# Adding the own part of a graph layer in PSUM after the division, with deeper buffers and a larger allowance in the instruction planner

## Chip, cores, metric

One core of a Trainium2 chip (trn2). The metric is the device time of one execution in microseconds (us).

## The reference, cut to what matters

The network has 32 graphs of 512 nodes with 128 features. `adj` is 0/1, symmetric, with ones on the diagonal. Four layers follow one another, each on a layer norm and ReLU of `x`, each added to `x`: masked attention (layer 0), a graph convolution whose weights come from an LSTM of 128 steps (layer 1), a four-step message passing (layer 2), and a linear graph layer (layer 3).

```python
# layer 2, one of four steps; input of step 2: [f2, f1]; of step 3: [f3, f1, f0]
src_agg  = einsum('bjv,bij->biv', nodes @ ws + bs, _l2norm(adj, 2))
dst_agg  = einsum('bjv,bji->biv', nodes @ wd + bd, _l2norm(adj, 1))
self_rep = nodes @ wn + bn                      # the "own" part
return tanh(concatenate([src_agg, self_rep, dst_agg], 2) @ wu + bu)
```

As `adj` is symmetric and 0/1, both aggregations divide by the same norm, the root of the degree. The kernel folds `ws`, `wd`, `wn` with `wu` at the start, so a step is `tanh(A y / norm + own + bias)`, where `A y` is the aggregation and `own` one product with a folded weight.

## The kernel before

The kernel records every operation with a rank, its reads, its writes and a guess of its duration. A planner then simulates the engines and fixes the order in which each engine gets its instructions. This order is static, fixed when the kernel is built. An engine's wait for the next one in line shows in the trace as idle time: in the kernel before, TensorE's waits came to 55.2 us in 50 cases between 620 and 1600 us. The planner adds an allowance between a producer on one engine and its consumer on another: `HOP`, or `HOP_PE` where the consumer is TensorE. LSTM steps have ranks below `URGENT` and a fixed small allowance of their own.

```python
class Plan:
    HOP, HOP_PE, HOP_URGENT, URGENT = 0.25, 0.8, 0.14, 1000
    # in put(o), for each engine e that can do operation o:
    hop = self.HOP_URGENT if o.rank < self.URGENT else self.HOP_PE if e == "PE" else self.HOP
    o.ready[e] = max([0.0] + [d.end + (hop if d.engine != e else 0.0) + d.gap for d in o.deps])

BUFS = {"a": 2, "ar": 4, "x": 5, "xn": 4, "y": 6, "gs": 4, "norm0": 3, "norm1": 3,
        "n0": 3, "n1": 3, "n2": 3, "n3": 3, "m0": 3, "m1": 3, "m2": 3, ...}
# tags in this list hand out their buffers in the order in which tiles were made:
plan = Plan(BUFS, ("ar", "x", "norm0", "norm1", "n0", "n1", "n2", "n3", "m0", "m1", "a"))
```

Pass 1 does the attention of the last 128 nodes of each graph (ranks from 10,000). The LSTM then runs with pass 2, the attention of the other nodes, beside it (20,000). The "rest" is layers 1 to 3 (30,000). Keys and queries wait in DRAM between pass 1 and pass 2. Layer 2 of one batch:

```python
for i, nch in enumerate(L2_CHUNKS):                    # 1, 1, 2, 3 chunks
    m = new(f"m{min(i, 2)}", (P, N), ...)
    DVE(..., nc.vector.tensor_mul(m.t, nodes[i].t, norm_row.t))   # node x norm
    ...  # py = bias + nodes @ folded weight; parts = py split into two fp32r parts
    def own():                                          # first into the bank
        for c, n in order[1:] + order[:1]:
            nc.tensor.matmul(pa.t, wf[:, W_F[i] + c, 1, :], scaled[n].t, start=..., stop=False)
    PE(R, nch * t_mm(N), own, [scaled[n] for n in CHUNKS[i]], [pa])
    def got():                                          # aggregation, eight matmuls
        ...  nc.tensor.matmul(pa.t, parts.t[:, j, k, :], ar.t[:, j, :], start=False, ...)
    PE(R, 8 * t_r(N), got, [parts, ar], [pa])
    DVE(R, t_dve(N), ... nc.vector.tensor_mul(pa.t, pa.t, inv_row.t))     # x 1/norm
    ACT(R, 0.5, ... tanh(pa + bias))
```

## Time and profile before

| | us |
|---|---|
| median of 4 runs | 1697.99 (1695.79 to 1701.61) |
| pass 1 ends (its last f_seq starts) | 251.6 |
| last LSTM tanh | 614.7 |
| last matmul of pass 2 (f_po) | 606.2 |
| granted TensorE clock, whole run | 0.981 |

The prediction below shows the lines that it rests on. Here are the stages, with borders at the end of pass 1 and at the last tanh of the LSTM. The columns are: stretch, length, busy us (and instructions) of PE (TensorE matmuls), PEld (its weight loads), DVE (VectorE), ACT (ScalarE) and POOL (GpSimd), granted clock, DMA share, GB/s. The tile names in later lines: f_pa is the PSUM bank in which aggregation and own part meet, f_py the product of nodes and folded weight, f_y its split parts, f_n the tanh, f_nb the row of norms, f_ar the squared adjacency; f_pf and f_hT_d belong to layer 3, f_po to pass 2, f_z, f_th and f_seq to the LSTM.

```profile
0.00:251.60 251.60, 213.58 (x1372) 171.19 (x1373) 139.86 (x648) 132.67 (x256) 86.88 (x240) 0.99 0.62 202
251.60:614.70 363.10, 358.04 (x2434) 301.93 (x2433) 200.19 (x958) 125.60 (x393) 53.34 (x103) 0.98 0.56 166
614.70:1694.80 1080.10, 1006.13 (x6147) 810.13 (x6147) 649.02 (x1787) 468.29 (x1079) 177.25 (x345) 0.98 0.14 44
700.00:1560.00 860.00, 813.40 (x5000) 655.31 (x5001) 522.11 (x1428) 386.22 (x891) 145.35 (x284) 0.99 0.15 47
```

The last row is the steady part of the rest. A batch has 193 TensorE instructions there (counted in the program), so 5000 of them in 860 us make one batch per 860 x 193 / 5000 = 33.2 us. I use this rate below, with 189 instructions for kernels that have the change.

### The profile page before, as it was taken

To read this page: it belongs to the slowest core of one execution; us is meant where nothing else is said; L and a number is where in the kernel's file an instruction comes from. 1 tells how busy PE (TensorE), PEld (TensorE's weight loads), DVE (VectorE), ACT (ScalarE), POOL (GpSimd) and SP (SyncE) were. 2 spreads that over 40 slices of the span, in tenths; PEclk is the share of its full clock that TensorE was granted. 3 is DMA by queue.
4 is the path that set the end of the run, shared out by engine and by line. 5 is a ranking of instruction groups with operands and counts; after the bars stand their busy time and mean duration, and the time that the engine had idled before them with its cause. 6 is when DMAs were issued, how large, how long until landed. Compare 5 with 4: busy or idle time off the path is not lost. (4 is left out here: it accounts for less than half of the span.)

```text
span 1694.8 us, 27758 instructions
## 1 busy us (share of the span) xinstructions
PE 1577.8 (93%) x9949; PEld 1283.3 (76%) x9949; DVE 989.1 (58%) x3392; ACT 726.6 (43%) x1727; POOL 317.5 (19%) x688
## 2 busy tenths in 40 slices
PE   5998999999999989999999899999999999999995
PEld 4777778888888878777777777777778777777774
DVE  4655655555555666566565665665756566565753
ACT  3565543333333354454444444444444444444431
POOL 3333321011111131121121111111211121121100
PEclk9999999999999989999999999999999999999997
DMA  7555665555555630111111111111301111011100
GB/s 254 188 186 175 199 214 175 157 163 155 162 156 157 200 130 26 38 51 38 63 50 38 63 38 50 63 38 38 100 13 38 50 63 63 13 50 38 38 7 15
DMA packets 144955, 159.06 MB, mean 94 GB/s; under 512 B 8612, under 2 KB 111140, under 8 KB 144808
## 3 DMA queue, kind: packets, MB, share of 16 engines
q1 hardware_dynamic: 143936, 155.42, 29.3%
q8 instruction: 80, 1.31, 0.3%
q10 hardware_dynamic: 872, 1.78, 0.3%
q14 instruction: 67, 0.55, 0.1%
HBM read 117.26 MB, written 39.91 MB: 93 GB/s over the span
## 5 line engine op out<-in xcount | busy, mean ns | idle before, releaser
L1283 PE MATMUL f_pa<-f_ar,f_y 128*128 128x512 f32 x1024 | 285.0, 421 | 13.9 <-DVE f_y L1156 9.5
L1283 PEld LDWEIGHTS f_pa<-f_ar,f_y 128*128 128x128 f32 x1024 | 188.1, 189 | 84.7 <-issue 23.7
L1276 PE MATMUL f_pa<-f_m,f_wf 128*128 128x512 f32 x448 | 215.8, 600 | 1.1 <-DVE f_m L1259 0.6
L1267 PE MATMUL f_py<-f_wf,f_n 128*128 128x128 f32 x1280 | 175.8, 276 | 10.5 <-ACT f_n L1287 10.4
L1267 PEld LDWEIGHTS f_py<-f_wf,f_n 128*128 128x128 f32 x1280 | 165.0, 192 | 19.8 <-ACT f_n L1287 14.0
L1287 ACT ACTIVATE f_n<-f_pa,f_bcol 128x512 f32<-128x512 f32 x128 | 87.7, 686 | 205.8 <-DVE f_pa L1285 205.8
L1085 PEld LDWEIGHTS f_z<-f_seq,f_w 128*128 128x128 f32 x1016 | 126.2, 194 | 26.5 <-DVE f_seq L1106 22.2
L1085 PE MATMUL f_z<-f_seq,f_w 128*128 128x32 f32 x1016 | 134.8, 277 | 5.1 <-DVE f_seq L1106 3.3
L1156 DVE TENSOR_TENSOR f_y<-f_py,f_y 128x512 fp32r<-128x512 f32 x128 | 87.8, 687 | 81.4 <-ACT f_y L1155 81.1
L1285 DVE TENSOR_TENSOR f_pa<-f_pa,f_norm 128x512 f32<-128x512 f32 x128 | 88.6, 693 | 79.3 <-PE f_pa L1283 79.2
L943 ACT ACTIVATE f_xn_c<-f_x,f_sh_c,f_rs_c 128x128 f32<-128x128 f32 x118 | 53.1, 487 | 156.4 <-DVE f_sh_c L948 138.8
L1276 PEld LDWEIGHTS f_pa<-f_m,f_wf 128*128 128x128 f32 x448 | 76.7, 193 | 50.8 <-issue 46.4
L1138 PE MATMUL f_po<-f_v,f_e 128*128 128x129 f32 x768 | 115.1, 285 | 0.0
L1138 PEld LDWEIGHTS f_po<-f_v,f_e 128*128 128x128 f32 x768 | 101.7, 195 | 11.5 <-PE f_s L1128 0.4
L1128 PE MATMUL f_s<-f_q,f_k 128*128 128x384 f32 x256 | 102.2, 498 | 0.5 <-PE f_pd L1054 0.5
L1155 ACT CAST f_y<-f_py 128x512 fp32r<-128x512 f32 x128 | 74.0, 579 | 59.4 <-PE f_py L1267 59.3
L1259 DVE TENSOR_TENSOR f_m<-f_n,f_norm 128x512 f32<-128x512 f32 x96 | 66.0, 687 | 42.9 <-ACT f_n L1287 42.9
L1089 ACT ACTIVATE f_th<-f_z 128x128 f32<-128x128 f32 x128 | 35.4, 277 | 129.5 <-PE f_z L1085 125.0
L1237 DVE SCALAR_TENSOR_TENSOR f_junk<-f_a,f_aT 128x512 bf16<-128x512 f32 x128 | 86.5, 675 | 1.6
L1132 DVE TENSOR_TENSOR f_e<-f_e,f_a 128x384 f32<-128x384 f32 x128 | 69.0, 548 | 30.5 <-ACT f_e L1131 29.8
L1267 PE MATMUL f_py<-f_wf,f_hT_c 128*128 128x128 f32 x512 | 83.3, 275 | 0.0
L1096 DVE SCALAR_TENSOR_TENSOR f_cu<-f_th,f_c 128x32 f32<-128x32 f32 x127 | 24.4, 192 | 99.2 <-ACT f_th L1089 98.5
(189 smaller groups left out, 3118.8 us busy)
## 6 DMA issues: line engine op xcount, KB each, us to landing
f_a<-in_adj_dram SPq DMA_DIRECT2D x32, 1024.0 KB, 5.1
f_a<-in_adj_dram SPq DMA_DIRECT2D x32, 768.0 KB, 5.6
f_dv<-f_v SPq DMA_DIRECT2D x32, 258.0 KB, 3.6
f_v<-f_dv SPq DMA_DIRECT2D x32, 258.0 KB, 2.8
f_x<-in_x_dram SPq DMA_DIRECT2D x32, 256.0 KB, 3.1
f_al<-in_adj_dram SPq DMA_DIRECT2D x32, 256.0 KB, 3.2
f_dk<-f_kT SPq DMA_DIRECT2D x32, 256.0 KB, 3.2
f_k<-f_dk SPq DMA_DIRECT2D x32, 256.0 KB, 2.7
```

Source lines behind the costliest of these rows:

```text
L1085: nc.tensor.matmul(z.t[:, k, q, :], w[:, W_HH + q, :], seq[:, t - 1, :], start=False, stop=True, skip_group_check=True)
L1128: PE(R, t_mm(NR), lambda s=s, j=j: nc.tensor.matmul(s.t, kT.t[:, bass.ts(j, P)], qT.t, start=True, stop=True), [kT, qT], [s])
L1132: DVE(R, t_dve(NR), lambda e=e, j=j: nc.vector.tensor_mul(e.t, e.t, a.t[:, j, :]), [a], [e])
L1138: nc.tensor.matmul(po.t[:, t, :], es[j].t[:, bass.ts(t, P)], v.t[:, j, :], start=(j == 0), stop=(j == NT - 1))
L1155: ACT(rank, t_act(N), lambda: nc.scalar.copy(parts.t[:, :, 0, :], src.t), [src], [(parts, 0)])
L1156: DVE(rank, t_dve(N), lambda: nc.vector.tensor_sub(parts.t[:, :, 1, :], src.t, f32(parts.t[:, :, 0, :])), [src, (parts, 0)], [(parts, 1)])
L1237: DVE(R + 2, 0.7, lambda tp=tp, j=j: nc.vector.scalar_tensor_tensor(junk, a.t[:, j, :], 1.0, flat(tp.t), OP.mult, OP.not_equal, accum_out= ...
L1267: nc.tensor.matmul(py.t[:, j, :], nodes[n].t[:, bass.ts(j, P)], wf[:, W_F[i] + c, 0, :], start=False, stop=(c == nch - 1), skip_group_chec ...
L1276: nc.tensor.matmul(pa.t, wf[:, W_F[i] + c, 1, :], scaled[n].t, start=(c == (1 if len(order) > 1 else 0)), stop=False)
L1283: nc.tensor.matmul(pa.t, parts.t[:, j, k, :], ar.t[:, j, :], start=False, stop=(k == 1 and j == NT - 1))
L1285: DVE(R, t_dve(N), lambda pa=pa: nc.vector.tensor_mul(pa.t, pa.t, inv_row.t), [inv_row], [pa])
L1287: ACT(R, 0.5, lambda pa=pa, n=n, i=i: nc.scalar.activation(n.t, pa.t, AF.Tanh, bias=bcol[:, i : i + 1]), [pa], [n])
```

## The change

The intent: skip the products of every node with the norm by adding the own part to what VectorE has divided, give the freed space to deeper buffers, and plan with more slack. Its core:

```diff
-    HOP, HOP_PE, HOP_URGENT, URGENT = 0.25, 0.8, 0.14, 1000
+    HOP, HOP_PE, HOP_URGENT, URGENT = 0.25, 1.2, 0.14, 1000
-    BUFS = {"a": 2, "ar": 4, "x": 5, "xn": 4, "y": 6, "gs": 4, "norm0": 3, "norm1": 3, "n0": 3, ... "m0": 3, "m1": 3, "m2": 3, ...
+    BUFS = {"a": 2, "ar": 5, "x": 6, "xn": 5, "y": 7, "gs": 5, "inv": 4, "n0": 4, "n1": 4, "n2": 4, "n3": 4, ...
@@ pass 1 and pass 2: keys and queries in one tile, in the buffers "ar" of the squared adjacency
-        qT = new("m0", (P, N), f"f_qT_{b}")
-        kT = new("m1", (P, N), f"f_kT_{b}")
+        kq = new("ar", (P, 2, N), f"f_kq_{b}")
-        DMA(R + 5, 192, lambda: nc.sync.dma_start(dq.t, qT.t[:, :NR]), [qT], [dq])
-        DMA(R + 5, 256, lambda: nc.sync.dma_start(dk.t, kT.t), [kT], [dk])
+        DMA(R + 5, 448, lambda: nc.sync.dma_start(dkq.t, flat(kq.t)[:, : N + NR]), [kq], [dkq])
@@ layer 2
-            DVE(R, t_dve(N), lambda m=m, i=i: nc.vector.tensor_mul(m.t, nodes[i].t, norm_row.t), ...)
-            PE(R, nch * t_mm(N), own, [scaled[n] for n in CHUNKS[i]], [pa])
             PE(R, 8 * t_r(N), got, [parts, ar], [pa])          # now opens the bank
             DVE(R, t_dve(N), lambda pa=pa: nc.vector.tensor_mul(pa.t, pa.t, inv_row.t), [inv_row], [pa])
+            def own(pa=pa, i=i, nch=nch):
+                for c, n in enumerate(CHUNKS[i]):
+                    nc.tensor.matmul(pa.t, wf[:, W_F[i] + c, 1, :], nodes[n].t, start=False, stop=(c == nch - 1), ...)
+            PE(R, nch * t_mm(N), own, [nodes[n] for n in CHUNKS[i]], [pa])
```

Cut: the norm row itself (4 transposes, one eviction, two GpSimd operations per batch), pass 2 reading the merged tile, and scratch of the weight folding moved from the norm buffers to "gs".

More of the change, by code (lines that the diff above doesn't have):

```diff
@@ L702, in symmetric @@
     assert D == P and N == 512
-    BUFS = {"a": 2, "ar": 4, "x": 5, "xn": 4, "y": 6, "gs": 4, "norm0": 3, "norm1": 3, "n0": 3, "n1": 3, "n2": 3, "n3": 3,
-            "m0": 3, "m1": 3, "m2": 3, "low": 3, "hp": 2, "x3": 2, "mm": 8, "st": 4, "mv": 4, "rs": 4, "sh": 4, "dg": 4, "dv": 4,
+    BUFS = {"a": 2, "ar": 5, "x": 6, "xn": 5, "y": 7, "gs": 5, "inv": 4, "n0": 4, "n1": 4, "n2": 4, "n3": 4, "low": 3, "hp": 2, "x3": 2, "mm": 8, "st": 4, "mv": 4, "rs": 4, "sh": 4, "dg": 4, "dv": 4,
             "ri": 3, "th": 3, "c": 3, "cu": 2, "cv": 2, "tcn": 2}
@@ L716, in symmetric @@
     sb = Buffered()
-    plan = Plan(BUFS, ("ar", "x", "norm0", "norm1", "n0", "n1", "n2", "n3", "m0", "m1", "a"))
+    plan = Plan(BUFS, ("ar", "x", "inv", "n0", "n1", "n2", "n3", "a"))
     def flat(ap):
@@ L826, in in_parts @@
     def in_parts(rank, n, m, dst, src, masks, r, wr, name):
-        hi = new("norm0", (n, m), f"f_bhi_{name}", FR)
-        lo = new("norm1", (n, m), f"f_blo_{name}")
+        hi = new("gs", (n, m), f"f_bhi_{name}", FR)
+        lo = new("gs", (n, m), f"f_blo_{name}")
         def fn():
@@ L880, in fold @@
             PE(FOLD, 3 * T_TR, turn, [w2], [tp])
-            wt = new("norm0", (P, 3, P), f"f_wTs_{i}_{c}")
+            wt = new("gs", (P, 3, P), f"f_wTs_{i}_{c}")
             ACT(FOLD, 0.5, lambda tp=tp, wt=wt: nc.scalar.copy(wt.t, tp.t), [tp], [wt])
@@ L896, in fold @@
         PE(FOLD, 3 * T_TR, turn_b, [rowb], [bt_ps])
-        bt = new("norm0", (P, 3, P), f"f_bTs_{i}")
+        bt = new("gs", (P, 3, P), f"f_bTs_{i}")
         ACT(FOLD, 0.5, lambda: nc.scalar.copy(bt.t, bt_ps.t), [bt_ps], [bt])
@@ L983, in pass_1 @@
         hT = ln_t(R, xn, "n0", f"a{b}")
-        qT = new("m0", (P, N), f"f_qT_{b}")
-        kT = new("m1", (P, N), f"f_kT_{b}")
-        for dst, m, c in ((qT, W_Q, C_Q), (kT, W_K, C_K)):
+        kq = new("ar", (P, 2, N), f"f_kq_{b}")
+        for k, m, c in ((0, W_K, C_K), (1, W_Q, C_Q)):
             pq = bank(f"f_pq_{b}_{m}")
@@ L989, in pass_1 @@
             plan.op({
-                "ACT": (0.5, lambda pq=pq, dst=dst, c=c: nc.scalar.activation(dst.t, pq.t, AF.Relu, bias=colb[:, c : c + 1])),
-                "DVE": (t_dve(N), lambda pq=pq, dst=dst, c=c: nc.vector.tensor_scalar(dst.t, pq.t, colb[:, c : c + 1], 0.0,
-                                                                                     OP.add, OP.max)),
-            }, R, [pq], [dst])
+                "ACT": (0.5, lambda pq=pq, k=k, c=c: nc.scalar.activation(kq.t[:, k, :], pq.t, AF.Relu, bias=colb[:, c : c + 1])),
+                "DVE": (t_dve(N), lambda pq=pq, k=k, c=c: nc.vector.tensor_scalar(kq.t[:, k, :], pq.t, colb[:, c : c + 1], 0.0,
+                                                                                 OP.add, OP.max)),
+            }, R, [pq], [(kq, k)])
         v = new("n3", (P, NT, P + 1), f"f_v_{b}")
@@ L1004, in pass_1 @@
         evict(R, N, lambda: v.t[:, :, :P], lambda: pv.t, [pv], [(v, "v")], relu=True)
-        dq = plan.fixed(dram.tile([P, NR], FP, tag=f"q{b}", name=f"f_dq_{b}"))
-        dk = plan.fixed(dram.tile([P, N], FP, tag=f"k{b}", name=f"f_dk_{b}"))
+        dkq = plan.fixed(dram.tile([P, N + NR], FP, tag=f"k{b}", name=f"f_dkq_{b}"))
         dv = plan.fixed(dram.tile([P, NT, P + 1], FP, tag=f"v{b}", name=f"f_dv_{b}"))
@@ L1010, in pass_1 @@
         dx = plan.fixed(dram.tile([P, L, P], FP, tag=f"x{b}", name=f"f_dx_{b}"))
-        kept[b] = (dq, dk, dv, dl, dx)
-        DMA(R + 5, 192, lambda: nc.sync.dma_start(dq.t, qT.t[:, :NR]), [qT], [dq])
-        DMA(R + 5, 256, lambda: nc.sync.dma_start(dk.t, kT.t), [kT], [dk])
+        kept[b] = (dkq, dv, dl, dx)
+        DMA(R + 5, 448, lambda: nc.sync.dma_start(dkq.t, flat(kq.t)[:, : N + NR]), [kq], [dkq])
         DMA(R + 5, 258, lambda: nc.sync.dma_start(dv.t, v.t), [v], [dv])
@@ L1019, in scores @@
             for t in range(NT):
-                nc.tensor.matmul(s.t[:, t, :], kT.t[:, bass.ts(t, P)], qT.t[:, NR:], start=True, stop=True)
-        PE(R, 4 * t_mm(P), scores, [kT, qT], [s])
+                nc.tensor.matmul(s.t[:, t, :], kq.t[:, 0, bass.ts(t, P)], kq.t[:, 1, NR:], start=True, stop=True)
+        PE(R, 4 * t_mm(P), scores, [kq], [s])
         e = new("n2", (P, NT, P), f"f_el_{b}")
@@ L1113, in pass_2 @@
         R = 20_000 + b * 10
-        dq, dk, dv, dl, dx = kept[b]
+        dkq, dv, dl, dx = kept[b]
         a = new("a", (P, NT, NR), f"f_a_{b}")
-        qT = new("m0", (P, NR), f"f_q2_{b}")
-        kT = new("m1", (P, N), f"f_k2_{b}")
+        kq = new("ar", (P, N + NR), f"f_kq2_{b}")
         v = new("n3", (P, NT, P + 1), f"f_v2_{b}")
         xc = new("x", (P, L, P), f"f_x2_{b}")
-        DMA(R, 256, lambda: nc.sync.dma_start(kT.t, dk.t), [dk], [kT])
-        DMA(R, 192, lambda: nc.sync.dma_start(qT.t, dq.t), [dq], [qT])
+        DMA(R, 448, lambda: nc.sync.dma_start(kq.t, dkq.t), [dkq], [kq])
         DMA(R, 768, lambda: nc.sync.dma_start(a.t, adj[b, :, :NR].rearrange("(t p) j -> p t j", p=P)), [], [a])
@@ L1127, in pass_2 @@
             s = bank(f"f_s_{b}_{j}", (P, NR))
-            PE(R, t_mm(NR), lambda s=s, j=j: nc.tensor.matmul(s.t, kT.t[:, bass.ts(j, P)], qT.t, start=True, stop=True),
-               [kT, qT], [s])
-            e = new(f"n{j}" if j < 3 else "m2", (P, NR), f"f_e_{b}_{j}")
+            PE(R, t_mm(NR), lambda s=s, j=j: nc.tensor.matmul(s.t, kq.t[:, bass.ts(j, P)], kq.t[:, N:], start=True, stop=True),
+               [kq], [s])
+            e = new(f"n{j}" if j < 3 else "gs", (P, NR), f"f_e_{b}_{j}")
             ACT(R, t_act(NR), lambda s=s, e=e: nc.scalar.activation(e.t, s.t, AF.Exp), [s], [e])
@@ L1161, in rest @@
         R = 30_000 + b * 10
-        dq, dk, dv, dl, dx = kept[b]
+        dkq, dv, dl, dx = kept[b]
         a = new("a", (P, NT, N), f"f_a3_{b}")
@@ L1172, in rest @@
                                                           accum_out=deg.t[:, t : t + 1]), [a], [(ar, t), (deg, t)])
-        dinv = new("dv", (P, 4, NT), f"f_dinv_{b}")
+        dinv = new("dv", (P, 3, NT), f"f_dinv_{b}")
         l1 = lns[b]
@@ L1180, in norms @@
             nc.gpsimd.tensor_scalar_max(d[:, 1, :], deg.t, 1.0)
-            nc.gpsimd.tensor_copy(d[:, 3, :], d[:, 1, :])
             nc.gpsimd.tensor_tensor(d[:, 0:2, :], d[:, 0:2, :], neg_half, OP.pow)
             nc.gpsimd.tensor_scalar_mul(d[:, 2, :], d[:, 0, :], 0.5)
-            nc.gpsimd.tensor_mul(d[:, 3, :], d[:, 3, :], d[:, 1, :])
             nc.gpsimd.tensor_mul(rs.t, ln1[:, b, 1, :], d[:, 0, :])
-        POOL(R, 3.2, norms, [deg, l1], [dinv, rs])
+        POOL(R, 2.7, norms, [deg, l1], [dinv, rs])
         sh = new("sh", (P, NT), f"f_sh_c{b}")
@@ L1239, in rest, with spread @@
                 [a, tp], [])
-        rows_of = []
-        for k in range(2):
-            tp = bank(f"f_nb_{b}_{k}", (P, NT, P))
-            def spread(tp=tp, k=k):
-                for t in range(NT):
-                    nc.tensor.transpose(tp.t[:, t, :], dinv.t[:, 1 + 2 * k, t : t + 1].to_broadcast([P, P]), ident)
-            PE(R + 1, 4 * T_TR, spread, [dinv], [tp])
-            r = new(f"norm{k}", (P, N), f"f_norm{k}_{b}")
-            evict(R + 1, N, lambda r=r: r.t, lambda tp=tp: flat(tp.t), [tp], [r])
-            rows_of.append(r)
-        inv_row, norm_row = rows_of
+        tp = bank(f"f_nb_{b}", (P, NT, P))
+        def spread(tp=tp):
+            for t in range(NT):
+                nc.tensor.transpose(tp.t[:, t, :], dinv.t[:, 1, t : t + 1].to_broadcast([P, P]), ident)
+        PE(R + 1, 4 * T_TR, spread, [dinv], [tp])
+        inv_row = new("inv", (P, N), f"f_inv_{b}")
+        evict(R + 1, N, lambda: inv_row.t, lambda tp=tp: flat(tp.t), [tp], [inv_row])
         nodes = [ln_t(R, xn, "n0", f"c{b}")]
-        scaled = []
         for i, nch in enumerate(L2_CHUNKS):
-            m = new(f"m{min(i, 2)}", (P, N), f"f_m{i}_{b}")
-            DVE(R, t_dve(N), lambda m=m, i=i: nc.vector.tensor_mul(m.t, nodes[i].t, norm_row.t), [nodes[i], norm_row], [m])
-            scaled.append(m)
             py = bank(f"f_py_{b}_{i}", (P, NT, P))
@@ L1271, in rest @@
             pa = bank(f"f_pa_{b}_{i}")
-            def own(pa=pa, i=i):
-                order = list(enumerate(CHUNKS[i]))
-                for c, n in order[1:] + order[:1]:
-                    nc.tensor.matmul(pa.t, wf[:, W_F[i] + c, 1, :], scaled[n].t, start=(c == (1 if len(order) > 1 else 0)),
-                                     stop=False)
-            PE(R, nch * t_mm(N), own, [scaled[n] for n in CHUNKS[i]], [pa])
             def got(pa=pa, parts=parts):
@@ L1282, in got @@
                     for j in range(NT):
-                        nc.tensor.matmul(pa.t, parts.t[:, j, k, :], ar.t[:, j, :], start=False, stop=(k == 1 and j == NT - 1))
+                        nc.tensor.matmul(pa.t, parts.t[:, j, k, :], ar.t[:, j, :], start=(k == 0 and j == 0),
+                                         stop=(k == 1 and j == NT - 1))
             PE(R, 8 * t_r(N), got, [parts, ar], [pa])
             DVE(R, t_dve(N), lambda pa=pa: nc.vector.tensor_mul(pa.t, pa.t, inv_row.t), [inv_row], [pa])
+            def own(pa=pa, i=i, nch=nch):
+                for c, n in enumerate(CHUNKS[i]):
+                    nc.tensor.matmul(pa.t, wf[:, W_F[i] + c, 1, :], nodes[n].t, start=False, stop=(c == nch - 1),
+                                     skip_group_check=True)
+            PE(R, nch * t_mm(N), own, [nodes[n] for n in CHUNKS[i]], [pa])
             n = new(f"n{i + 1}" if i < 3 else "gs", (P, N), f"f_n{i + 1}_{b}")
```

## The prediction

> **What bounds the kernel now.** I read the page's busy shares first, then the 40 slices, then a table of busy time by stage, then what TensorE itself waited for in the longest stage, and last the rows of the instructions that the change touches.
>
> ```profile
> PE 1577.8 (93%) x9949; PEld 1283.3 (76%) x9949; DVE 989.1 (58%) x3392; ACT 726.6 (43%) x1727; POOL 317.5 (19%) x688
> PE   5998999999999989999999899999999999999995
> DMA  7555665555555630111111111111301111011100
> ```
>
> TensorE is busy nearly everywhere. No other engine passes 60%, and the DMA engines are all but idle in the second half. So what TensorE executes, and the holes it cannot fill, set the time. The columns of the next rows are the stretch, its length, and busy us of PE, PEld, DVE, ACT and POOL, then clock, DMA share and GB/s.
>
> ```profile
> 50.00:250.00 200.00, 180.68 (x1177) 145.62 (x1177) 113.84 (x521) 112.45 (x218) 67.92 (x190) 0.99 0.59 191
> 250.00:620.00 370.00, 362.41 (x2456) 305.73 (x2454) 203.43 (x971) 128.15 (x401) 56.17 (x110) 0.97 0.56 166
> 620.00:1600.00 980.00, 927.18 (x5725) 748.42 (x5726) 603.70 (x1671) 442.10 (x1025) 169.36 (x330) 0.99 0.14 47
> 1600.00:1695.00 95.00, 76.17 (x415) 59.52 (x414) 43.67 (x108) 24.14 (x48) 5.06 (x8) 0.88 0.04 13
> ```
>
> I chose the borders by where the tiles begin and end. The first row is pass 1. The second is the LSTM with pass 2 beside it: its steps (18 tanh per 50 us, so 2.8 us each) go on whatever else is done, and TensorE is idle 8 of 370 us. The third is the "rest" (layers 1 to 3), where nearly the whole change lies: 53 of 980 us idle. The fourth is the tail with 19 us idle. In the third, TensorE waited for (us in total, times, longest):
>
> ```profile
> PE f_pf L1305 <- ACT f_hT_d L771: 16.1, 10, 2.3
> PE f_pa L1283 <- DVE f_y L1156: 9.5, 10, 1.8
> PE f_py L1267 <- ACT f_n L1287: 9.1, 9, 1.5
> PE f_n4T L1293 <- ACT f_n L1287: 6.2, 5, 1.3
> PE f_pa L1283 <- ACT f_y L1155: 4.4, 6, 1.2
> ```
>
> There is no single slow producer. There are some 50 short waits (sum of all rows there 55 us, so 1.1 us each) on ScalarE and VectorE results that came later than the order of instructions allowed. This order is fixed when the kernel is built, by a planner that assumes 0.8 us from any other engine to TensorE.
>
> [...] an aggregation matmul has a mean of 421 ns, yet eight of them start within 1.86 us. I therefore cost TensorE by start-to-start times, and the 53 us idle is a lower bound. [...] transposes in a stream here start 0.11 us apart, which is what one costs.
>
> **The change, part by part.** The algebra: (norm times own + aggregation) times 1/norm becomes aggregation times 1/norm, plus own.
>
> ```profile
> L1276 PE MATMUL f_pa<-f_m,f_wf 128*128 128x512 f32 x448 | 215.8, 600 | 1.1 <-DVE f_m L1259 0.6
> L1249 PE MATMUL f_nb<-f_ident,f_dinv 128*128 128x128 f32 x256 | 35.9, 276 | 0.0
> L1259 DVE TENSOR_TENSOR f_m<-f_n,f_norm 128x512 f32<-128x512 f32 x96 | 66.0, 687 | 42.9 <-ACT f_n L1287 42.9
> L1259 DVE TENSOR_TENSOR f_m<-f_hT_c,f_norm 128x512 f32<-128x512 f32 x32 | 21.8, 682 | 5.9 <-ACT f_hT_c L771 5.9
> ```
>
> Removed from TensorE: the norm row, 4 of 8 transposes per batch, so 128 x 0.11 = **14 us**. TensorE is the bound there, so all of it counts. The own part itself stays: 448 records, 14 per batch, 0.43 us apart.
>
> Removed from VectorE: all 128 products, 66.0 + 21.8 = 88 us, and half of 11 evictions of 0.68, 4 us. About 29 of 32 batches lie in the third stage, so its VectorE load falls from 604 to about 520 us (62% to 53%). ScalarE loses half of 53 evictions of 0.60 us, 16 us. GpSimd loses two small operations per batch (0.19 and 0.20 us). None of these bounds, so none counts by itself. They count by results that arrive on time.
>
> Holes in the third stage: visible 53 us. For hidden ones: a batch costs TensorE, by start-to-start times, 4 aggregations x 1.86 + 28 x 0.22 (f_py) + 7 x 0.86 (own) + about 10.8 for all else = 30.4 us. The stage ran 5725 of 193 instructions per batch, 29.7 batches, so 902 us of work in 980: some 25 us more, of which the clock of 0.99 takes 9. The planner's allowance rises from 0.8 to 1.2 us, so each of 50 waits can shrink by up to 0.4 us: 20 us at most. I take 14, as some waits are shorter and some orders will change. A fourth batch (ar 4 to 5, nodes 3 to 4 buffers) gives the planner work to put in, and a VectorE with 14% less to do is less late: another 10 from the visible and 4 from the hidden part, a guess within these sizes. Together **28 us**.
>
> Pass 1: its two largest waits are f_pol for f_el, 10.9 us in 13 times, and f_pq for f_hT_a, 4.6 in 7. Twenty waits x 0.4 would be 8; I take **6 us**. Keys and queries now share one buffer of five and one transfer instead of two: 64 transfers fewer in all, hidden, with DMA engines 59% busy. They take their turn behind the five weight loads of the same tag, so the folding of weights moves into the head, where TensorE waits 16.4 us for the bias rows anyway: 0.
>
> LSTM stage: 0, as its chain and its priority are not touched.
>
> Against it: own now stands after the division in each layer's chain. In steady state other batches cover it. For the last batch nothing does. In its last layer own ran while the split went on:
>
> ```profile
> 1664.36 2.58 PE f_pa L1276 x6
> 1666.94 1.88 PE f_pa L1283 x8
> 1668.84 0.71 DVE f_pa L1285
> ```
>
> Now the split (0.59 + 0.69 us) stands bare and own's 2.58 us follow the division: about 1.4 us longer there, and as much in the layers before where little else is left. **+3 us**.
>
> Sum: 1697.8 - 14 - 28 - 6 + 3 = **1653 us**, 2.7% less.
>
> **Rivals.** (A) The waits move. With own behind the division TensorE could stand for f_pa's VectorE product 128 times instead. For: this product is late already (79 us idle before it, though for TensorE). Against: VectorE is then only half busy, and the planner puts 1.2 us between. Then holes stay at 53, and only the transposes and part of pass 1 count: 1675 to 1685. (B) VectorE was the hidden cause of most waits. For: f_y and f_pa products sit in every layer's chain and f_m went out among them. Against: the largest wait, for f_hT_d, ends with ScalarE. Then 50 of the 78 us of lost time return: about 1630. (C) Eight PSUM banks, not SBUF buffers, limit the batches in flight, and longer planned hops hold banks longer. About 22 banks per 33 us, held 3 to 8 us each, is 3 in use on average, so I doubt it; it would give about 1680 to 1700. (D) The weight folding at the head blocks pass 1 by a few us: +5.
>
> **Range and chances.** The transposes are sure, the rest depends on the planner. All holes unchanged and the tail longer: 1687. Half of all lost time back: about 1635. I take 1630 to 1680 for 8 in 10. Faster by 2% means under 1664, that is 20 us or more from holes net of the tail, against 31 in my sum: chance 0.66. Within 2%: 0.31. Slower by 2% would need a new bound, of which I see no sign: 0.03.
>
> **What would show it.** Right: 128 f_nb records in place of 256, no f_m; TensorE idle in the middle under 35 us; waits of f_pf and f_pa each shorter; VectorE about 53% in the rest; pass 1 ending some 6 us sooner, the LSTM equally long. Wrong: waits of the own matmuls for the division among the top rows (A), waits for a free bank or idle as large as before (C), pass 1 ending later (D).

## The result, and the profile after

The changed kernel took 1670.39 us (median of 4 runs, 1668.39 to 1680.99) against 1697.99: ratio 0.9845, 95% interval 0.9807 to 0.9884. A ratio is the mean time of one kernel's runs over that of the other's in the same rounds, so not quite the ratio of the medians. The gain is 1.6%, 28 us where 45 were predicted, inside the range.

The page's first lines for the changed kernel:

```profile
PE 1574.6 (94%) x9821; PEld 1290.5 (77%) x9821; DVE 913.3 (54%) x3288; ACT 705.0 (42%) x1671; POOL 305.9 (18%) x624
PEclk9999998999999898999999999999999999999997
```

128 TensorE instructions fewer, as forecast; VectorE 76 us less (913.3 against 989.1), where 92 were forecast. The stages, cut at the same two events (256.8 and 632.4 us now):

```profile
0.00:256.80 256.80, 215.00 (x1375) 171.92 (x1376) 145.24 (x668) 124.33 (x238) 87.06 (x240) 0.98 0.61 201
256.80:632.40 375.60, 368.37 (x2368) 313.40 (x2368) 192.79 (x927) 118.69 (x373) 53.16 (x90) 0.92 0.53 154
632.40:1679.20 1046.80, 991.19 (x6082) 805.21 (x6081) 575.25 (x1693) 461.94 (x1060) 165.68 (x294) 0.98 0.15 47
700.00:1560.00 860.00, 837.38 (x5158) 679.89 (x5157) 479.73 (x1398) 391.59 (x895) 137.94 (x243) 0.99 0.15 48
```

Read it row by row against the rows of before. Pass 1 is 5.2 us longer, the LSTM stage 12.5 us longer at a clock of 0.92 in place of 0.98, and the rest 33.3 us shorter: 5.2 + 12.5 - 33.3 = -15.6 us, the difference of the two profiled spans (1679.2 against 1694.8). The median gain is larger, as the profiled run was the longest of its kernel (1680.99 us at a clock of 0.965; its other runs took 1668 to 1671 at 0.970 to 0.974). In the steady rest TensorE idles 22.6 of 860 us in place of 46.6, and a batch takes 860 x 189 / 5158 = 31.5 us in place of 33.2. So the rest gained 33.3 us, against 39 in the forecast (14 + 28 - 3), and some 18 us were given back before it began.

What TensorE waited for between 620 and 1600 us (total us, times, longest), which answers to the five rows in the prediction:

```profile
PE f_pa L1267 <- DVE f_pa L1263: 5.2, 10, 0.8
PE f_nb L1239 <- POOL f_dinv L1175: 4.7, 2, 2.8
PE f_pa L1260 <- DVE f_junk L1229: 3.8, 1, 3.8
PE f_aT L1227 <- ACT f_ar L1165: 3.3, 4, 2.3
PE f_py L1251 <- ACT f_n L1271: 3.1, 2, 2.1
```

The new wait, own (L1267) for the division (L1263), heads the list, but with 5.2 us in 10 cases; all waits of this stretch sum to 33.9 us in 38 cases, where they were 55.2 in 50. The old leaders have shrunk: f_pf for f_hT_d from 16.1 to 1.2 us. The second and fourth rows are new. They fall at the start of the rest, where layer 1 of the first batch was formerly prepared while the LSTM still ran. The first and last starts of the squaring of the adjacency show it (before, then after; ns min/median/max, then the us of first and last):

```profile
L1171 ACT ACTIVATE f_ar<-f_a x128: 614/621/664, 599.6 to 1580.5; 128x512 fp32r<-128x512 f32 x128
```

```profile
L1165 ACT ACTIVATE f_ar<-f_a x128: 612/620/676, 633.5 to 1540.2; 128x512 fp32r<-128x512 f32 x128
```

Before, it began 15 us ahead of the last LSTM tanh (614.7); after, 1 us behind it (632.4). Pass 2 had ended later too: its last matmul started at 635.7 in place of 606.2.

### The profile page after: what moved, and what is told of

It is laid out like the page before. It is cut to its first block, busy times and chain, and to the rows that moved or that the text cites. A ratio compares the mean times of both kernels' runs of the same rounds, so it can differ in the third digit from the quotient of the medians.

```text
span 1679.2 us, 27052 instructions
## 1 busy us (share of the span) xinstructions
PE 1574.6 (94%) x9821; PEld 1290.5 (77%) x9821; DVE 913.3 (54%) x3288; ACT 705.0 (42%) x1671; POOL 305.9 (18%) x624
## 4 chain that ended last, share of the span: by engine, by line
PE 66%; DVE 12%; POOL 7%; ACT 7%; DMA 5%; issue 3%; SPq 0%; ACTq 0%; POOLq 0%; DVEq 0%
PE f_pa L1260 11%; PE f_pa L1267 9%; PE f_py L1251 8%; PE f_z L1081 8%; PE f_s L1122 5%; PE f_po L1132 4%; PE f_pg L1300 3%; PE f_pg L1196 2%; ACT f_ar L1165 2%; POOL f_dinv L1175 2%; DMA f_x<-in_x_dram 2%; DMA f_a<-in_adj_dram 2%; PE f_z L1075 2%; PE f_pf L1289 2%; PE f_pq L986 1%
## 5 line engine op out<-in xcount | busy, mean ns | idle before, releaser
L1260 PE MATMUL f_pa<-f_ar,f_y 128*128 128x512 f32 x1024 | 272.8, 411 | 10.1 <-ACT f_y L1149 4.0
L1251 PEld LDWEIGHTS f_py<-f_wf,f_n 128*128 128x128 f32 x1280 | 165.7, 192 | 15.4 <-ACT f_n L1271 5.2
L1267 PE MATMUL f_pa<-f_n,f_wf 128*128 128x512 f32 x320 | 154.1, 597 | 4.4 <-DVE f_pa L1263 4.4
L1081 PEld LDWEIGHTS f_z<-f_seq,f_w 128*128 128x128 f32 x1016 | 132.7, 202 | 32.6 <-DVE f_seq L1102 27.4
L1081 PE MATMUL f_z<-f_seq,f_w 128*128 128x32 f32 x1016 | 139.0, 282 | 7.2 <-DVE f_seq L1102 5.4
L1263 DVE TENSOR_TENSOR f_pa<-f_pa,f_inv 128x512 f32<-128x512 f32 x128 | 88.3, 692 | 78.0 <-PE f_pa L1260 78.0
L1132 PE MATMUL f_po<-f_v,f_e 128*128 128x129 f32 x768 | 122.2, 302 | 0.0
L1132 PEld LDWEIGHTS f_po<-f_v,f_e 128*128 128x128 f32 x768 | 109.6, 211 | 9.0
L1122 PE MATMUL f_s<-f_kq 128*128 128x384 f32 x256 | 104.6, 522 | 0.0
L1267 PEld LDWEIGHTS f_pa<-f_n,f_wf 128*128 128x128 f32 x320 | 55.9, 190 | 45.9 <-issue 36.1
L1165 ACT ACTIVATE f_ar<-f_a 128x512 fp32r<-128x512 f32 x128 | 79.3, 624 | 6.3 <-DMA f_a<-in_adj_dram 6.3
```

Source lines behind the costliest of these rows:

```text
L1081: nc.tensor.matmul(z.t[:, k, q, :], w[:, W_HH + q, :], seq[:, t - 1, :], start=False, stop=True, skip_group_check=True)
L1122: PE(R, t_mm(NR), lambda s=s, j=j: nc.tensor.matmul(s.t, kq.t[:, bass.ts(j, P)], kq.t[:, N:], start=True, stop=True), [kq], [s])
L1132: nc.tensor.matmul(po.t[:, t, :], es[j].t[:, bass.ts(t, P)], v.t[:, j, :], start=(j == 0), stop=(j == NT - 1))
L1165: ACT(R, 0.62, lambda t=t: nc.scalar.activation(ar.t[:, t, :], a.t[:, t, :], AF.Square, accum_out=deg.t[:, t : t + 1]), [a], [(ar, t), (de ...
L1251: nc.tensor.matmul(py.t[:, j, :], nodes[n].t[:, bass.ts(j, P)], wf[:, W_F[i] + c, 0, :], start=False, stop=(c == nch - 1), skip_group_chec ...
L1263: DVE(R, t_dve(N), lambda pa=pa: nc.vector.tensor_mul(pa.t, pa.t, inv_row.t), [inv_row], [pa])
```

## The experiments

Twelve runs, each timed in three rounds against the kernel before on the same chip. All gave correct results, so adding on top of a bank that VectorE has rewritten gave a correct result in each of the eleven that have the change (all but e3). All of them in one table; the stage columns are from each one's profile, the clock is that of its timed and profiled runs.

| kernel | us, median | ratio to before | pass 1 ends | LSTM ends | rest, us | us per batch | clock |
|---|---|---|---|---|---|---|---|
| before | 1697.99 | 1 | 251.6 | 614.7 | 1080.1 | 33.2 | 0.981-0.987 |
| changed | 1670.39 | 0.9845 | 256.8 | 632.4 | 1046.8 | 31.5 | 0.965-0.974 |
| e1 algebra alone | 1676.78 | 0.9890 | 253.4 | 613.4 | 1062.0 | 32.3 | 0.983-0.987 |
| e2 algebra, 1.2 us | 1699.76 | 1.0028 | 268.8 | 634.3 | 1062.8 | 31.9 | 0.975-0.976 |
| e3 before, 1.2 us | 1732.56 | 1.0232 | 268.8 | 628.8 | 1098.8 | 33.4 | 0.961-0.966 |
| e4 changed, 0.8 us | 1672.01 | 0.9859 | 253.9 | 616.8 | 1054.9 | 31.9 | 0.980-0.983 |
| e5 changed, 1.2 us in the rest only | 1653.80 | 0.9750 | 253.5 | 614.2 | 1035.5 | 31.5 | 0.980-0.984 |
| e6 as e5, last four batches 0.8 us | 1657.03 | 0.9770 | 254.7 | 617.7 | 1038.3 | 31.5 | 0.981-0.985 |
| e7 as e4, keys and queries apart | 1660.35 | 0.9785 | 254.2 | 614.3 | 1044.4 | 31.6 | 0.985-0.986 |
| e8 changed, node buffers as before | 1675.00 | 0.9867 | 264.5 | 621.5 | 1050.3 | 31.6 | 0.974-0.979 |
| e9 e5 and e7 together | 1660.92 | 0.9799 | 254.3 | 615.6 | 1043.8 | 31.6 | 0.981-0.987 |
| e10 as e9, 1.6 us in the rest | 1659.18 | 0.9787 | 253.8 | 615.0 | 1043.5 | 31.6 | 0.983-0.989 |
| e11 e1 with idle products | 1665.00 | 0.9819 | 252.8 | 618.3 | 1051.3 | 31.9 | 0.984-0.990 |
| e12 changed, again | 1670.13 | 0.9834 | 257.3 | 633.7 | 1046.2 | 31.5 | 0.968-0.980 |

### First call: the parts by themselves

**e1**, the algebra with everything else as before (`inv` in the old "norm0" buffers):

```diff
-        rows_of = []  ...  inv_row, norm_row = rows_of          # two rows
+        inv_row = new("norm0", (P, N), f"f_inv_{b}")            # one row
-            DVE(... tensor_mul(m.t, nodes[i].t, norm_row.t) ...)   PE(own)   PE(got)   DVE(divide)
+            PE(got)   DVE(divide)   PE(own)
```

> The algebra alone: own part after the division, no norm row, no products; old buffers, old allowance of 0.8 us, keys and queries where they were. Theory 1 (each part of the change gives its share; the algebra is worth its 14 us of transposes plus a little from a relieved VectorE): 1675 to 1685 us, pass 1 ending near 252 us and the LSTM near 615 as in the kernel before. Rival (the algebra needs the fourth batch, because own now waits for the division): TensorE waits of own for the division of 20 us or more and a time of 1690 or more. Second rival (relief of VectorE is the true gain): 1665 or less, with the holes in the rest halved.

Measured 1676.78 us, 18.7 less than before (1695.51 in these rounds). Own waited for the division 10.3 us in 14 cases in the steady stretch:

```profile
PE f_pa L1273 <- DVE f_pa L1269: 10.3, 14, 1.7
```

The time lies where the first theory put it, and the rival that the algebra needs a fourth batch is out: it asked for waits of 20 us or more.

**e2**, the same with the allowance:

```diff
-    HOP, HOP_PE, HOP_URGENT, URGENT = 0.25, 0.8, 0.14, 1000     # in e1
+    HOP, HOP_PE, HOP_URGENT, URGENT = 0.25, 1.2, 0.14, 1000
```

> The algebra and the allowance of 1.2 us, old buffers. Theory 1: another 10 to 15 us less than the algebra alone in the rest stage (waits shrink by up to 0.4 us each), so about 1665 to 1672. If the allowance of 1.2 us is also what slows the end of pass 2 and the LSTM stage, the LSTM ends 10 us or more later than 615 here too, and the sum gains little. If that loss comes from keys and queries in the shared buffers instead, the LSTM ends near 615 and this kernel is at least as fast as the changed one (1670).

A miss: 1699.76 us, 23 us more than e1. Pass 1 ends 15.4 us later and the LSTM 20.9 us later, and the keys and queries are in their old buffers here. So the allowance, not the shared buffers, delays the first two stages. Of the 20.9 us only 5.5 arise in the LSTM stage itself (365.5 us long against 360.0). The rest is no shorter than in e1 (1062.8 against 1062.0): the 10 to 15 us that the allowance was to gain there did not come.

**e3**, the kernel before with that one constant:

```diff
-    HOP, HOP_PE, HOP_URGENT, URGENT = 0.25, 0.8, 0.14, 1000
+    HOP, HOP_PE, HOP_URGENT, URGENT = 0.25, 1.2, 0.14, 1000
```

> The kernel before with nothing but the allowance at 1.2 us. Theory 1: holes in the rest from 53 to about 38 us, so 1680 to 1688. Rival (three batches in flight are too few to fill longer planned hops): holes unchanged or more, 1695 to 1710. LSTM stage: as in the run with the algebra, later by 10 us if the allowance is the cause.

1732.56 us, 37 us more; the rival's direction, and further. Its first two stages:

```profile
0.00:268.80 268.80, 220.09 (x1367) 173.88 (x1368) 148.48 (x676) 122.66 (x230) 86.02 (x240) 0.97 0.58 191
268.80:628.80 360.00, 355.16 (x2377) 303.23 (x2377) 192.26 (x929) 117.75 (x372) 52.89 (x90) 0.96 0.55 160
```

Pass 1 takes 17.2 us more for the same work (1367 records against 1372), the LSTM stage itself no more than before (360.0 against 363.1), and the rest 18.7 more (1098.8 against 1080.1). For pass 1 I give this reason: the planner holds every matmul that another engine feeds back by 0.4 us more in its own time; with three buffers it has nothing to put in between, so it plans a longer pass 1. Running the planners of the two kernels without a chip bears it out for about half: pass 1 ends 8.0 us later in the plan, with TensorE idle 7.7 us longer. For much of the other 9 us the clock is the likely reason: in pass 1 TensorE was at half clock for 17.1 us, against 3.4 before, which would cost some 7 us (an estimate: half of the difference; e12 shows how it is read).

**e4**, the changed kernel with the old allowance:

```diff
-    HOP, HOP_PE, HOP_URGENT, URGENT = 0.25, 1.2, 0.14, 1000     # in the changed kernel
+    HOP, HOP_PE, HOP_URGENT, URGENT = 0.25, 0.8, 0.14, 1000
```

> The changed kernel with the allowance put back to 0.8 us. Theory 1: the rest stage loses its shorter waits, plus 10 to 15 us there. If the allowance is what delays pass 2 in the LSTM stage, that stage gets its 12 us back and the total stays about 1665 to 1675. If the shared buffers delay it, the LSTM still ends near 630 and the total is 1680 or more.

1672.01 us, the same as the changed kernel. The total hides two effects of opposite sign, which the stages show:

```profile
253.90:616.80 362.90, 354.89 (x2428) 299.18 (x2426) 201.11 (x962) 126.93 (x396) 54.85 (x106) 0.99 0.54 164
616.80:1671.70 1054.90, 992.15 (x6014) 800.36 (x6014) 560.01 (x1642) 462.10 (x1056) 156.92 (x278) 0.98 0.14 45
```

At 0.8 us the LSTM ends 15.6 us sooner than in the changed kernel, and the rest is 8.1 us longer. (These are profiled runs, and the changed kernel's took 10.6 us more than its median, so the 15.6 is more than its usual run would show.) So 1.2 us seems to pay in the rest and to cost before it.

### Second call: the allowance by stage, the layout

**e5**:

```diff
+    HOP, HOP_PE, HOP_URGENT, URGENT = 0.25, 0.8, 0.14, 1000
+    HOP_PE_REST = 1.2
-                hop = self.HOP_URGENT if o.rank < self.URGENT else self.HOP_PE if e == "PE" else self.HOP
+                hop = (self.HOP_URGENT if o.rank < self.URGENT else self.HOP if e != "PE"
+                       else self.HOP_PE_REST if o.rank >= 30_000 else self.HOP_PE)
```

> The changed kernel with the allowance of 1.2 us for the rest stage alone, 0.8 us for pass 1, pass 2 and the LSTM. Theory now: the allowance pays in the steady rest (per batch 31.97 to 31.40 us there, so some 18 us on 32 batches) and costs in pass 1 (3 us), at the end of pass 2 and the LSTM (some 15 us later) and in the drain. Then pass 1 ends near 254, the LSTM near 615, and the time is 1652 to 1664. Rival (the allowance itself is worth nothing, and the two allowances merely give two orders of equal worth by chance): 1668 to 1675.

1653.80 us, inside the expected 1652 to 1664: the best of all kernels here, 0.9750 of before (0.9732 to 0.9769), and some 17 us under the changed kernel.

```profile
0.00:253.50 253.50, 215.03 (x1382) 172.74 (x1383) 145.20 (x666) 125.81 (x240) 86.50 (x240) 0.97 0.63 206
253.50:614.20 360.70, 354.45 (x2428) 298.36 (x2426) 201.17 (x962) 127.19 (x396) 55.02 (x106) 0.99 0.55 166
614.20:1649.70 1035.50, 982.23 (x6014) 794.92 (x6014) 562.78 (x1653) 456.23 (x1045) 159.14 (x278) 0.98 0.14 46
```

The first two stages are as long as those of the kernel before within 2.4 us, with the clock within 0.02, and the rest is 44.6 us shorter than before. What the changed kernel gave back is recovered by this one condition. At the same allowance in the rest, and the same 31.5 us per batch, the rest is 11.3 us shorter than the changed kernel's: pass 2 is done at 601.0, and the squaring of the first adjacency starts at 592.1, 22 us ahead of the last tanh.

**e6** returned the last four batches of the rest to 0.8 us:

```diff
-                       else self.HOP_PE_REST if o.rank >= 30_000 else self.HOP_PE)
+                       else self.HOP_PE_REST if 30_000 <= o.rank < 30_280 else self.HOP_PE)
```

> As the run before it, and the last four batches of the rest back at 0.8 us, for the drain. Theory: the drain after the last steady batch gets shorter by 3 to 8 us, so 3 to 8 us less than with 1.2 us in the whole rest. Rival (the drain is the last batch's own chain, which no order changes): the same within 2 us.

1657.03 us, 3.2 more than e5 and not 3 to 8 less. The drain does not respond as I thought. But 3.2 us is no clear difference either (the intervals of the two ratios overlap), and the profile of e6 shows as much before the rest begins (617.7 against 614.2), where the matmuls of both follow in the same order.

**e7** gave keys and queries two buffers of their own, at 0.8 us throughout:

```diff
-    BUFS = {"a": 2, "ar": 5, "x": 6, ...
+    BUFS = {"a": 2, "ar": 4, "kq": 2, "x": 6, ...
-        kq = new("ar", (P, 2, N), f"f_kq_{b}")          # also in pass 2
+        kq = new("kq", (P, 2, N), f"f_kq_{b}")
```

> The changed kernel at 0.8 us with keys and queries in two buffers of their own instead of the five shared ones (four left there; the same bytes). Rival to the allowance theory: sharing makes pass 1 wait for the weight loads and the rest wait for pass 2; then pass 1 ends 2 to 4 us sooner than 253.9, the first aggregation starts sooner than 606.5, and the time falls to about 1665. Theory: sharing costs nothing, 1669 to 1676.

1660.35 us, 11.7 less than e4: my theory that sharing costs nothing missed. But the reason of the rival missed too. Pass 1 ends at 254.2 against 253.9, and the first aggregation starts at 610.1, later than the 606.5 of e4. Of the gain, 10.5 us lie in the rest (1044.4 against 1054.9), where keys and queries no longer exist and this kernel has one buffer fewer for the squared adjacency. Much of it may be the clock, which e12 takes up below: TensorE ran at half clock for 24.8 us of the rest, against 51.3 in e4, which is worth some 13 us (an estimate: half of the difference). Why the clock was better is open.

**e8** put the node buffers and some others back:

```diff
-    ... "x": 6, "xn": 5, "y": 7, "gs": 5, "inv": 4, "n0": 4, "n1": 4, "n2": 4, "n3": 4, ...
+    ... "x": 5, "xn": 4, "y": 6, "gs": 5, "inv": 3, "n0": 3, "n1": 3, "n2": 3, "n3": 3, ...
```

> The changed kernel (1.2 us) with three node buffers, three inverse rows, five x, four xn and six y as in the kernel before; the five shared buffers stay. Depth is worth 30 us at 1.2 us (1700 with all old buffers against 1670) and only 5 at 0.8 us. If the fourth batch's node buffers carry that, this run is 1690 to 1700, with pass 1 ending near 268 us and the drain long. If the shared buffers carry it, it stays at 1670 to 1676.

1675.00 us; the rest takes 1050.3 against 1046.8, and pass 1 lasts 7.7 us longer. So the fourth node buffer is worth little in the rest. It helps pass 1 to bear the allowance: 268.8 with all old buffers (e2), 264.5 here, 256.8 in the changed kernel. The time lies where the second case put it, so most of the 30 us between e2 and the changed kernel goes with what stayed here: the fifth "ar" and "gs" and the merged keys and queries. And with 1.2 us throughout the LSTM stage itself takes 357.0 us here, where it takes 375.6 in the changed kernel:

```profile
264.50:621.50 357.00, 352.22 (x2353) 298.73 (x2352) 191.36 (x922) 119.62 (x374) 52.88 (x90) 0.97 0.54 159
```

So the allowance alone does not lengthen that stage; it did so together with the deeper node buffers.

### Third call: do the gains add, and what is chance

**e9** joins e5 and e7, **e10** is e9 with 1.6 us:

```diff
-    HOP_PE_REST = 1.2      # e9
+    HOP_PE_REST = 1.6      # e10
```

> Both repairs at once: keys and queries in two buffers of their own (worth 12 us at 0.8 us) and the allowance of 1.2 us in the rest stage alone (worth 17 us against 1.2 everywhere, 18 against 0.8 everywhere). If the two gains have different causes they add: 1642 to 1648. If both come from the same thing (a fuller order in the rest, by whichever means), they do not add: 1652 to 1660.

> As the run before it with 1.6 us in the rest. If waits are hidden by the allowance in proportion, the steady rest gains a little more and the drain loses as much: within 5 us of the run before it. If three to four batches no longer fill the longer planned hops, 10 us or more slower, as 1.2 us was with the old buffers.

1660.92 and 1659.18 us. The gains do not add: with the own buffers for keys and queries the allowance in the rest is worth nothing (e7, e9 and e10 lie within 2 us), with the shared ones it is worth 18 (e4 to e5). All of these reach 31.5 to 31.6 us per batch. The rate looks like what several orders come to, not like a sum of separate causes.

**e11** put 128 products back on VectorE in e1, node times the inverse row into a tile that nobody reads:

```diff
+            m = new(f"m{min(i, 2)}", (P, N), f"f_m{i}_{b}")
+            DVE(R, t_dve(N), lambda m=m, i=i: nc.vector.tensor_mul(m.t, nodes[i].t, inv_row.t), [nodes[i], inv_row], [m])
```

> The algebra alone (1676.8 us) with 128 products put back on VectorE: each node times the inverse row into a tile that nobody reads, so VectorE has its old load and TensorE its new one. If relief of VectorE is a part of the gain of 18.7 us, the time rises by about 5 us or more (1681 and up), with more waits of TensorE on VectorE results. If the 128 transposes are all of it, it stays within 2 us of 1676.8.

1665.00 us, 11.8 us **less** than e1 (11.1 when each is set against the kernel before on its own chip), with 58 us more VectorE work. Neither of the two cases came true. Its steady rest:

```profile
700.00:1560.00 860.00, 831.33 (x5097) 667.39 (x5096) 527.80 (x1462) 411.95 (x952) 145.70 (x246) 1.00 0.15 49
```

VectorE is as busy there as in the kernel before (527.8 against 522.1 us), yet a batch takes 31.9 us in place of 33.2. So the gain does not need a relieved VectorE. And useless work that gains 12 us can hardly have done so but by giving the planner another order (of the rest alone: up to the end of the LSTM both kernels have the same order of matmuls). This sets a scale for everything above: two orders of almost the same work can differ by some 12 us for no reason that I can name (a different clock is one part of it), so differences of that size between two kernels, e7's included, are not proof of the cause they were made for.

**e12** is the changed kernel again.

> The changed kernel unaltered, for a second profile: its first one fell in the longest of its runs (1681 against 1668 to 1671), with a granted clock of 0.92 in the LSTM stage and that stage 371 us long. If the low clock belongs to the order of instructions, it is below 0.95 here too; if it was chance, the stage is some 10 us shorter at a clock near 0.97, pass 1 and the rest being the same within 2 us. Time 1668 to 1672.

1670.13 us, and the stages repeat: pass 1 to 257.3, the LSTM to 633.7 at a clock of 0.92.

```profile
257.30:633.70 376.40, 368.31 (x2367) 313.90 (x2367) 192.99 (x927) 118.97 (x373) 53.48 (x90) 0.92 0.52 154
```

So a low clock goes with this order. How low is less sure: both profiled runs were the longest of their four, and the others had a better clock over the whole run. The four runs of e12 also show what the clock is worth: 1681.68 us at 0.968, 1674.48 at 0.971, 1665.78 at 0.976, 1660.79 at 0.980. From the first to the last the clock differs by 0.012, which on 1670 us is 20 us, the whole of their difference (20.9). Three slices of the LSTM stage, first in the changed kernel (its first profile), then in e5:

```profile
310.00:330.00 20.00, 19.27 (x112) 16.10 (x111) 9.82 (x50) 5.50 (x18) 1.27 (x3) 0.84 0.36 102
390.00:410.00 20.00, 19.57 (x112) 16.23 (x112) 8.48 (x43) 6.04 (x19) 1.27 (x3) 0.83 0.43 116
550.00:570.00 20.00, 19.58 (x117) 16.79 (x116) 8.69 (x43) 5.78 (x19) 1.86 (x3) 0.83 0.44 130
```

```profile
310.00:330.00 20.00, 19.52 (x134) 16.19 (x132) 11.30 (x57) 6.29 (x21) 3.12 (x6) 1.00 0.63 192
390.00:410.00 20.00, 19.78 (x136) 16.51 (x134) 11.45 (x58) 6.61 (x21) 1.26 (x3) 1.00 0.45 139
550.00:570.00 20.00, 19.93 (x138) 16.95 (x139) 10.87 (x53) 6.81 (x22) 2.53 (x6) 1.00 0.59 171
```

TensorE counts as busy in both, but gets 112 to 117 instructions done in place of 134 to 138, at a clock of 0.83 to 0.84 in place of 1.00. The half clock is in the trace: the clock records of the kernel before and of the changed one hold no values but 1.0 and 0.5, and those at 0.5 last 3.41 us or a multiple, but for the last of each run (24.47 and 26.59 us). At half clock consecutive matmuls of f_po start 0.214 us apart, at full clock 0.112 (medians of 93 and 557 pairs in the changed kernel's trace), so nearly half of the time at half clock is lost where they follow one another. Over that kernel's whole LSTM stage 4.0 matmuls start per us at half clock and 6.7 at full, 40% fewer, so the estimates here that take half are upper ones. In the second slice the half clock is one stretch of 6.83 us. TensorE counts as busy for 3.04 of the 3.40 us before it, and its waits from 250 to 620 us sum to 5.4 us in 9 cases, the longest 2.8. What takes the clock down is not shown by these traces. The first row is the 3.40 us before, the second the stretch:

```profile
398.50:401.90 3.40, 3.04 (x25) 2.78 (x25) 0.80 (x6) 0.78 (x3) 0.00 (x0) 1.00 0.11 41
402.00:408.60 6.60, 6.60 (x26) 5.39 (x24) 2.70 (x15) 1.23 (x4) 0.00 (x0) 0.50 0.18 41
```

Across the runs the clock follows the allowance: kernels with 1.2 us outside the rest have 0.961 to 0.980, all the others 0.980 to 0.990. Summed over the LSTM stage, the half clock also goes with the length of that stage. In each row but e8's, the traces show the same order of matmuls up to the last tanh (in the first row for the first 3775 of some 3800):

| kernels | LSTM stage, us | of it at half clock, us |
|---|---|---|
| before, e1, e11 | 363.1, 360.0, 365.5 | 14.1, 6.8, 20.0 |
| e4, e5, e6 | 362.9, 360.7, 363.0 | 9.4, 8.1, 9.3 |
| e7, e9, e10 | 360.1, 361.3, 361.2 | 6.8, 10.2, 9.6 |
| e2, e3 | 365.5, 360.0 | 41.0, 30.7 |
| e8 | 357.0 | 23.9 |
| changed, e12 | 375.6, 376.4 | 58.0, 58.0 |

In the first and fourth row one and the same order varies by 5.5 us from run to run, about half of the difference of its time at half clock (13.2 and 10.3 us). In the two profiles of the changed kernel the stretches at half clock lie at the same places within 1.3 us, but for one that e12 has more and one that is shorter there. Its 43.9 us more of half clock than before cost some 22 us of TensorE time (an estimate: half of them; 18 at 40%), more than the 12.5 us by which its stage is longer. So the clock is enough to account for the longer stage.

## Why the prediction was right or wrong

**The result lies in the range, 17 us over the point, but the call that was thought likelier, faster by 2% or more (0.66), did not come true.** Two of the five terms were wrong, one in sign and one by being zero, and the reasons given for the largest do not hold one by one; that the range held is owed in part to its width of 50 us, and so to luck. By its own steps:

- *The transposes, 14 us*: the 128 records are gone. With the new wait small (5.2 us), they are the likeliest part of the gain of e1 (18.7 us). But nothing measured them alone, and 18.7 is not far above the 12 us scatter of orders.
- *Holes in the rest, 28 us*: right in direction. In the steady part it was too small: from 33.2 to 31.5 us per batch is 1.7 x 32 = 54 us with the transposes, against 42 predicted for both. But the whole stage gained only 33.3 us, as it began with work that was formerly done under the LSTM and ended with a longer tail. The waits named did shrink, and TensorE's visible idle time between 620 and 1600 us fell from 53 to 34 us. VectorE was busy 57% of it, not 53%. The reasons I gave did not hold one by one: relief of VectorE is not needed (e11); the fourth node buffer is worth about 3.5 us in the rest (e8); the allowance is worth 18 us with one layout and none with others (e4 to e5; e7 to e9, and the rest of e1 to e2).
- *Pass 1, minus 6 us*: wrong in sign, plus 5.2. I took the allowance as slack that hides waits. In the planner it is also time that must be filled. With too little in flight it is planned as a hole; the plan bears this out for about half of the loss in e3, and the clock is the likely reason of much of the other half. Undone alone, in e4, it gave back 2.9 of the 5.2 us. In the old buffers it costs 15 to 17 (e2, e3).
- *"LSTM stage: 0, as its chain and its priority are not touched"*: this is the step that failed most. It was 12.5 us longer. The chain was not touched, but the work beside it was: pass 2 was planned with the same longer hops, and TensorE's clock fell to 0.92, 58.0 us of the stage at half clock where it had been 14.1. Pass 2 also ended 29.5 us later and kept layer 1 of the first batch from starting under the LSTM, which the rest had to pay. e4 and e5 undo both with nothing but the allowance outside the rest; e8 undoes the longer stage with nothing but the old depth of the node buffers and some others (at the price of 7.7 us more in pass 1). So the cause is the order that the two gave together.
- *Tail, plus 3 us*: too small. From the start of the last bias matmul of f_py to the end it is 41.0 us (1638.2 to 1679.2) against 33.5 (1661.3 to 1694.8), so plus 7.5.
- *Rivals*: A (own waits for the division): its sign came true, as this wait heads the list, but 5.2 us in all and idle time of 34 in place of 53 us refute it. B (VectorE the hidden cause) is refuted by e11. C (PSUM banks) found little support: of the five top rows one, f_pa for f_junk, ends with a tile that the waiting matmul does not read, so it is probably a wait for a bank, 3.8 us in one case; in the other four it reads, or adds to, what it waits for. D (weight folding at the head): its sign, pass 1 ending later, came true, but not for its reason: pass 1 ends at 253.9 with shared buffers (e4) and 253.4 without (e1).

The sum closes in the profiled runs: 11.2 us missed in pass 1, 12.5 in the LSTM stage and 5.7 in the rest (33.3 in place of 39) are 29.4, and 45 - 29.4 = 15.6 us is the gain of the profiled spans. The medians miss by 17 only, as the changed kernel's profiled run was 10.6 us above its median. One sum of the prediction is also off: half of the 78 us of lost time back gives, with its other terms, 1642 and not about 1635.

**What stays open**: why the order planned with 1.2 us and the deeper buffers lowers the clock in the LSTM stage; how long that stage is in the changed kernel's usual runs, which had a better clock and no profile; and why e7 has a better clock in the rest. The first and last would need orders that differ in one place only, which this planner does not give.

## What to carry to other kernels

In this statically ordered program 0.4 us more slack between engines gained 18 us in all where the rest alone got it with one layout (e4 to e5), nothing with another (e7 to e9), and made pass 1 15 to 17 us longer in the old buffers (e2, e3), where the planner's own run had TensorE idle 7.7 us longer. So set slack by stage and check each stage's length, not the total or the end time alone. Before naming a cause for a gain of one per cent, disturb the order with work that cannot help (as e11 did) and see how far the time moves by itself. And look at the granted clock beside every run: here 0.012 of it was worth 20 us, where the change was worth 28, and one and the same order took 360.0 to 365.5 us for one stage.
